# Layer 0's second product in seven block products, with a hand-written order of all engines in that stage

## The chip, the cores and the metric

The kernel runs on one NeuronCore of one Trainium2 chip. The time is the device time of one execution in microseconds (us); a kernel is compared by the median of several executions. The profile records one further execution with the hardware profiler: every instruction of the matrix engine (PE, with its weight loads as PEld), the vector engine (DVE), the scalar engine (ACT), Pool (GpSimd) and the DMA issues of the sync engine's queue (SP). All data are float32.

## The reference, cut to what matters

Four graph layers follow one another over x of shape (128, 64, 256). Only layer 0 is touched:

```python
h = jnp.maximum(_layernorm(x), 0.0)              # 128 * 64 = 8192 rows of 256
agg = jnp.einsum('nm,bmd->bnd', A_hat, h)
x1 = agg.reshape(-1, 256)
h1 = relu(_batchnorm(x1 @ W1.T + b1, g1, be1))   # 512 channels; mean and variance over all rows
out = h1 @ W2.T + b2                             # 256 channels: the second product
out = _batchnorm(out, g2, be2)                   # mean and variance over all rows again
x = x + out.reshape(x.shape)
```

Both batch norms need the statistics of all 8192 rows before any row can go on. Layer 1 (a graph convolution and four LSTMs), layer 2 (attention) and layer 3 (attention with four heads) follow.

## The kernel before, in words

The 8192 rows are cut into 16 chunks of 512 (`CH = 512`, `NCH = 16`). In layer 0 the channels lie on the 128 partitions and the rows of a chunk along the free axis. `KH = 4` blocks of 128 channels make the 512 hidden channels, `KD = 2` make the 256 of the output.

The stage has two passes. In the first, `product1(c)` (line 349) computes z1 of chunk c: its lower two channel blocks go to a tile of the pool `res`, the upper two to a tile of the pool `z1b`; `st1` collects the statistics. Then `bn_params` (line 286) makes scale and shift `sc1`, `sh1`, one channel block after the other.

In the second pass `product2(chunks, by_block)` (line 366) does three things for a chunk: ACT applies scale, shift and relu to the four blocks of z1 into a tile `h1` (line 373; two buffers in the pool `l0b`); PE multiplies by `w2_sb`, two output blocks of four products each (line 377); DVE takes the statistics of each result from PSUM and then writes it to SBUF with the bias added (lines 381 and 382; the result overwrites the lower z1 tile, `z2[c] = lo`). Chunks 0 and 1 are done together, the products ordered by channel block, because their scale and shift come out one block after the other; chunks 2 to 15 one at a time. A float32 matmul of 128x128 weights and 512 columns leaves two records on PE in the trace.

Beside this pass the weights of later layers are prepared. `weight_sums(p, q)` (line 493) loads one of twelve sets of LSTM weights to SBUF (two DMAs on SP, two buffers), lets Pool form four sums or differences of 128x256 (line 502), and stores the set to DRAM (two DMAs, lines 504 and 505); it is called once before each of the chunks 2 to 13. `weight_transposes` (line 463) transposes the weights of layer 2 on PE before chunk 14; `weight_products` follows the last chunk. Then `bn_params` with `st2` makes `sc2`, `sh2`.

What comes next on SP: the weights of layer 1 (`wg0`, `wg1`, `wih1`), then six of the stored sets (`load_sets(6)`, line 549), then the x of chunks 0 and 1 (line 611). The tiles for these lie on the bytes of tiles that the second pass has finished with, `z1b` above all, so each load waits for the last reader of the bytes below it. `first_convolutions` (line 608) starts layer 1: ACT and DVE scale the first chunks with `sc2`, `sh2`, PE transposes them, and DVE adds the x that was loaded (line 622).

The order of the work: inside `tc.manual_schedule(engines=...)` the engines listed issue their instructions in the order of the program text. The other engines' order is made by a planner, which goes by its own estimate of when an instruction can start. Around the second pass only PE is in the list; DVE, ACT, Pool and SP are the planner's. `tc.no_sync_barrier()` is a fence for the planner: no instruction of any engine moves across it, and no engine waits at it. PSUM has eight banks here, one tag `ps`, handed out in turn.

In layer 3 the kernel already computes one product in seven block products (`seven`, line 1308; `sums_h`, line 1298; `ring_places`), with the helper `differences` (line 690): for two-by-two blocks of both factors, four differences on each side replace the eighth product. The LSTMs use the same scheme.

## Time and profile before

| | us |
|---|---|
| median of 5 runs | 1919.75 |
| lowest and highest | 1919.26, 1920.34 |
| the profiled execution's own time | 1919.35 |
| its span, first to last instruction | 1917.5 |

Where the second pass lies in that span, and how busy the engines are in it (us of each window; all at a granted PE clock of 1.00):

| window (us from the span's start) | what | PE | DVE | ACT | Pool |
|---|---|---|---|---|---|
| 157.70 to 171.43 | chunks 2 and 3 | 13.73 | 6.70 | 7.13 | 5.60 |
| 185.17 to 198.90 | chunks 6 and 7 | 13.73 | 5.40 | 5.86 | 6.17 |
| 226.37 to 240.10 | chunks 12 and 13 | 13.73 | 5.39 | 5.86 | 0.00 |
| 240.10 to 253.84 | transposes, chunk 14, most of 15 | 13.73 | 8.01 | 2.93 | 0.08 |

How to read it: the window's length is 13.73 us in each row, so PE has work all the time, and the others wait for it. The sum of an engine's busy time says nothing of the path that sets the end; the chain of waits does. Busy time of PE is modelled from start and size of its matmuls, so rates are better taken from the distance between starts.

### The profile page before, as it was taken

How to read it: one execution, taken by the hardware profiler on the slowest of the kernel's cores; microseconds unless marked ns; L12 is line 12 of the kernel's file. 1: busy time of each engine (PE TensorE's matmuls, PEld its weight loads, DVE VectorE, ACT ScalarE, POOL GpSimd, SP SyncE). 2: the span in 40 equal slices, each digit the busy share in tenths (PEclk: the TensorE clock that was granted, in tenths of full speed). 3: DMA queues.
4: the chain of work that ended last, by engine and by line, in shares of the span. 5: the costliest groups of instructions: out<-in, count | busy, mean ns of one | idle time of the engine just before them, and what ended most of it. 6: DMA issues, size and time to landing. Idle time of an engine off the chain costs nothing.

```text
span 1917.5 us, 38323 instructions
## 1 busy us (share of the span) xinstructions
PE 1898.3 (99%) x14981; PEld 1460.6 (76%) x14981; DVE 1158.2 (60%) x3020; ACT 958.7 (50%) x2132; POOL 414.8 (22%) x615
## 2 busy tenths in 40 slices
PE   9999999999999999999999999999999999999998
PEld 5444465897897889699689789879969967777776
DVE  6644354546557656755755665665555557777776
ACT  5654434445456455455545545545554544444453
POOL 4205210221211121122121121112112213233232
PEclk9999999999999999999999999999999999999999
DMA  4206712224524521532542452253144245444533
GB/s 138 67 32 224 279 49 67 83 83 161 159 83 146 180 99 58 179 105 94 186 144 83 160 182 84 75 197 111 55 160 127 92 131 156 133 142 147 144 111 111
DMA packets 110500, 240.35 MB, mean 125 GB/s; under 512 B 11377, under 2 KB 74353, under 8 KB 110321
## 3 DMA queue, kind: packets, MB, share of 16 engines
q1 hardware_dynamic: 109568, 236.57, 37.1%
q8 instruction: 118, 1.93, 0.4%
q0 software_dynamic: 320, 1.05, 0.2%
q14 instruction: 62, 0.50, 0.1%
q10 hardware_dynamic: 432, 0.30, 0.0%
HBM read 169.98 MB, written 67.90 MB: 124 GB/s over the span
## 4 chain that ended last, share of the span: by engine, by line
PE 94%; DVE 3%; ACT 1%; DMA 1%; issue 0%; POOL 0%; SPq 0%; DVEq 0%; ACTq 0%; POOLq 0%
PE x L848 23%; PE g L812 18%; PE z L848 11%; PE y L848 6%; PE z L377 6%; PE v L1120 6%; PE z L360 5%; PE p_q L1127 3%; PE u L593 3%; PE v L579 3%; PE X L1316 3%; PE Y L1316 1%; PE agg_c L214 1%; PE o L1241 1%; PE agg_b L214 1%; PE o L1443 1%
## 5 line engine op out<-in xcount | busy, mean ns | idle before, releaser
L857 DVE TENSOR_TENSOR gates<-gates,x 128x128 f32<-128x128 f32 (+2 forms) x384 | 119.5, 322 | 335.8 <-PE x L848 333.6
L848 PE MATMUL x<-xd,wset 128*128 128x128 f32 (+2 forms) x1280 | 285.0, 310 | 0.1
L848 PE MATMUL x<-hd,wset 128*128 128x128 f32 (+2 forms) x1152 | 246.7, 303 | 0.0
L906 POOL TENSOR_TENSOR gates<-gates 128x512 f32<-128x512 f32 (+2 forms) x48 | 75.0, 1562 | 647.9 <-ACT gates L740 647.9
L848 PEld LDWEIGHTS x<-xd,wset 128*128 128x128 f32 x1280 | 202.1, 190 | 16.9 <-DVE gates L857 3.0
L740 ACT ACTIVATE gates<-gates,bias 128x256 f32<-128x256 f32 (+4 forms) x384 | 170.4, 490 | 66.4 <-DVE gates L857 63.5
L848 PEld LDWEIGHTS x<-hd,wset 128*128 128x128 f32 x1152 | 185.1, 191 | 5.0
L791 ACT ACTIVATE gates<-g,bias 128x512 f32<-128x512 f32 (+2 forms) x240 | 138.2, 610 | 98.0 <-PE g L812 94.7
L812 PE MATMUL g<-hT,wset 128*128 128x256 f32 (+2 forms) x744 | 184.4, 405 | 1.1 <-DVE hT L751 1.1
L812 PEld LDWEIGHTS g<-hT,wset 128*128 128x128 f32 x744 | 140.5, 190 | 44.1 <-issue 8.8
L812 PE MATMUL g<-hT,wih 128*128 128x512 f32 x384 | 166.4, 592 | 0.0
L854 ACT COPY gates<-y 128x128 f32<-128x128 f32 (+2 forms) x192 | 54.2, 294 | 204.9 <-PE y L848 204.4
L848 PE MATMUL z<-hs,wset 128*128 128x128 f32 (+2 forms) x768 | 154.1, 303 | 0.0
L812 PEld LDWEIGHTS g<-hT,wih 128*128 128x128 f32 x384 | 72.3, 190 | 87.7 <-issue 83.2
L848 PEld LDWEIGHTS z<-hs,wset 128*128 128x128 f32 x768 | 119.8, 191 | 3.3
L360 PE MATMUL z<-agg,w_sb 128*128 128x512 f32 x256 | 114.1, 598 | 0.0
L797 DVE TENSOR_TENSOR cell<-gates 128x512 f32<-128x512 f32 (+2 forms) x80 | 50.6, 650 | 101.2 <-ACT gates L791 101.1
L377 PE MATMUL z<-h,w_sb 128*128 128x512 f32 x256 | 110.2, 592 | 0.0
L857 DVE TENSOR_TENSOR gates<-gates,z 128x128 f32<-128x128 f32 (+2 forms) x384 | 104.6, 316 | 0.1
L854 ACT COPY gates<-x 128x128 f32<-128x128 f32 (+2 forms) x192 | 56.6, 296 | 93.7 <-PE x L848 93.0
L740 ACT ACTIVATE gates<-x,bias 128x128 f32<-128x128 f32 (+2 forms) x192 | 74.8, 390 | 50.9 <-PE x L848 48.0
L848 PE MATMUL z<-hT,wset 128*128 128x128 f32 (+1 forms) x512 | 96.9, 301 | 0.0
(245 smaller groups left out, 3640.5 us busy)
## 6 DMA issues: line engine op xcount, KB each, us to landing
wset<-wfar SPq DMA_DIRECT2D x96, 960.0 KB, 6.4
hT<-far_h SPq DMA_DIRECT2D x124, 128.0 KB, 2.9
far_h<-hm SPq DMA_DIRECT2D x16, 512.0 KB, 4.1
far_n<-xs SPq DMA_DIRECT2D x16, 512.0 KB, 6.4
xs<-far_n SPq DMA_DIRECT2D x64, 128.0 KB, 3.6
far_x<-xs SPq DMA_DIRECT2D x16, 512.0 KB, 3.0
x<-far_x SPq DMA_DIRECT2D x64, 128.0 KB, 3.2
xt<-in_x_dram SPq DMA_DIRECT2D x15, 512.0 KB, 4.0
```

Source lines behind the costliest of these rows:

```text
L360: nc.tensor.matmul(ps, w1_sb[:, k, m * P : (m + 1) * P], agg[:, k, :], start=(k == 0), stop=(k == KD - 1))
L377: nc.tensor.matmul(banks[c, m], w2_sb[:, k, m * P : (m + 1) * P], h1[c][:, k, :], start=(k == 0), stop=(k == KH - 1))
L579: nc.tensor.matmul(banks[m], wg0_sb[:, k, m * P : (m + 1) * P], agg[:, k, :], start=(k == 0), stop=(k == KD - 1))
L740: nc.scalar.activation(gate(q, c, part), src, AF.Tanh if q == 2 else AF.Sigmoid, bias=bs[:, q * KD + c : q * KD + c + 1])
L791: nc.scalar.activation(columns_of(gate(q, c)), natural(banks[q, c][:, :n].rearrange("p (w b) -> p w b", b=nb)), AF.Tanh if q == 2 else AF. ...
L812: nc.tensor.matmul(banks[q, c][:, :n].rearrange("p (w b) -> p w b", b=nb)[:, w, :], block(q, c, k), hv[:, k, w.start * p : (w.stop - 1) * ...
L848: nc.tensor.matmul(folded(self.psum(kind)), wsets[p, self.q][:, BLOCKS[kind][i], :], (ox[self.s] if part == "x" else oh)[kind], start=firs ...
L854: nc.scalar.copy(gate(self.q, kind // 5, halves[kind // 5]), self.psum(kind))
L857: nc.vector.tensor_add(gate(self.q, *dst), gate(self.q, *a), self.psum(kind))
L906: nc.gpsimd.tensor_mul(gates[:, 0, :, :n], gates[:, 0, :, :n], gates[:, 2, :, :n])
L1120: nc.tensor.matmul(ps[:, i, :], hT[:, k, j, :], w[:, k, first : first + D], start=(k == 0), stop=(k == KD - 1))
L1316: nc.tensor.matmul(st[c, tag][:, i * CH // 2 : (i + 1) * CH // 2].rearrange("p (a n) -> p a n", n=P), w, st[c, "o7"][kind], start=first an ...
```

## The change

The second product of chunks 2 to 14 is computed in seven block products instead of eight. The two factors are cut in two by two blocks: the weights into two halves of the 512 hidden channels and two halves of the 256 outputs, the chunk into the two halves of the hidden channels and two halves of 256 rows. A block product has a depth of 256, so two matmuls of 128x128 weights and 256 columns.

- Four combinations of the weight blocks (`w2_sums`) are made once by Pool, in the first pass.
- For each chunk four differences of the blocks of h1, t1 to t4, each 128x512: three on DVE, t3 on Pool (the new argument `third` of `differences`).
- The relu is applied in place, to z1, by ACT (`relu`), no longer into an `h1` tile; the tile of the differences takes the `h1` tag's two buffers.
- The seven products go to three PSUM banks X, Y and Z of a chunk. X is summed on through products 1, 6, 7 and 4 and read after each (`copy` by ACT, `add` by DVE); Y takes products 5 and 3, Z takes 2.
- The statistics are taken from the SBUF result after the bias was added, so `bn_params` runs with `biased` true. Those of chunks 0 and 1 are taken in iterations 3 and 4.
- PE, DVE, ACT and Pool have a hand-written order in this stage, between two fences. Products 7 and 4 of a chunk stand among the first products of the next one. Weight transposes stand around the last two products of chunk 14.
- Chunk 15 keeps the old product, after the second fence; its relus stand on ACT at the end of iteration 14. SP is still the planner's, but its instructions don't cross the fences either.

The core of the diff:

```diff
+    def differences(engine, dst, b11, b12, b21, b22, third=None):
+        t1, t2, t3, t4 = dst
+        return [lambda: engine.tensor_tensor(t1, b12, b11, OP.subtract),
+                lambda: ((third or engine).tensor_tensor(t3, b22, b12, OP.subtract),
+                         engine.tensor_tensor(t2, b22, t1, OP.subtract)),
+                lambda: engine.tensor_tensor(t4, b21, t2, OP.subtract)]
...
-        for c in chunks:
-            for m in range(KD):
-                nc.vector.bn_stats(st2[:, m, c, :], banks[c, m])
-                nc.vector.tensor_scalar(z2[c][:, m, :], banks[c, m], bn2_sb[:, 0, m : m + 1], None,
-                                        op0=OP.add)
+        return banks
+
+    def result2(c, m, ps):
+        nc.vector.tensor_scalar(z2[c][:, m, :], ps, bn2_sb[:, 0, m : m + 1], None, op0=OP.add)
+
+    def stats2(c, m):
+        nc.vector.bn_stats(st2[:, m, c, :], z2[c][:, m, :])
...
+    class Seven2:
+        def __init__(self, c):
+            self.c, self.banks = c, {}
+            self.b = {(k, j): a[:, :, halves2[j]] for k, a in enumerate(z1whole[c]) for j in range(2)}
+
+        def relu(self, *ks):
+            for k in ks:
+                one = slice(k, k + 1)
+                nc.scalar.activation(z1[self.c][k], z1[self.c][k], AF.Relu, bias=sh1[:, one],
+                                     scale=sc1[:, one])
+
+        def begin(self):
+            b = self.b
+            t = l0b.tile([P, 4, KH // 2, CH // 2], F32, tag="h1", name=f"t2_{self.c}")
+            t = [t[:, i] for i in range(4)]
+            self.sums = differences(nc.vector, t, b[0, 0], b[0, 1], b[1, 0], b[1, 1], nc.gpsimd)
+            self.at = {1: b[0, 0], 2: b[1, 0], 3: b[1, 1], 4: t[3], 5: t[0], 6: t[1], 7: t[2]}
+
+        def product(self, kind, tag):
+            first = tag not in self.banks
+            if first:
+                self.banks[tag] = bank(f"{tag}2_{self.c}")[:, : CH // 2]
+            for k in range(KH // 2):
...
+                nc.tensor.matmul(self.banks[tag], w, right[:, k, :], start=first and not k, stop=True,
+                                 skip_group_check=True)
+
+        def copy(self, m, j, tag):
+            nc.scalar.activation(self.part(m, j), self.banks[tag], AF.Identity,
+                                 bias=bn2_sb[:, 0, m : m + 1])
+
+        def add(self, m, j, tag):
+            nc.vector.tensor_add(self.part(m, j), self.part(m, j), self.banks[tag])
+
+        def stats(self, m):
+            nc.vector.bn_stats(st2[:, m, self.c, :], z2[self.c][:, m, :])
...
+        w2_sums = l0b.tile([P, 4, KH // 2, P], F32, name="w2_sums", bufs=1)
...
+            nc.gpsimd.tensor_tensor(w2_sums[:, dst], u, v, op)
...
-        for c in range(2, NCH):
-            if c == NCH - 2:
-                weight_transposes()
+    tc.no_sync_barrier()
+    with tc.manual_schedule(engines={mybir.EngineType.PE, mybir.EngineType.DVE,
+                                     mybir.EngineType.Activation, mybir.EngineType.Pool}):
+        sevens = {c: Seven2(c) for c in range(2, NCH - 1)}
+        sevens[2].relu(2, 3, 0, 1)
+        for c in range(2, NCH - 1):
+            a, b, z = sevens[c], sevens.get(c + 1), sevens.get(c - 1)
             if wanted:
                 weight_sums(*wanted.pop(0))
-            product2([c], False)
-        sc2, sh2 = bn_params(st2, bn2_sb, const, "bn2", False)
+            a.product(2, "Z")
+            if c == 2:
+                a.begin()
+                for f in a.sums:
+                    f()
+                for m in range(KD):
+                    result2(0, m, banks[0, m])
+            if b:
+                b.relu(0)
+            if z:
+                z.product(7, "X")
+                z.add(1, 1, "X")
+            if b:
+                b.relu(1)
+            a.product(1, "X")
+            a.copy(0, 0, "X")
+            if z:
+                z.stats(0)
+            a.product(5, "Y")
+            a.copy(1, 1, "Y")
+            if b:
+                b.relu(2)
+            a.add(0, 0, "Z")
+            if c == 2:
+                for m in range(KD):
+                    result2(1, m, banks[1, m])
+            if z:
+                z.product(4, "X")
+                z.copy(1, 0, "X")
+            if b:
+                b.relu(3)
+                b.begin()
+                b.sums[0]()
+            if z:
+                z.stats(1)
+            a.product(6, "X")
+            a.copy(0, 1, "X")
+            if b:
+                b.sums[1]()
+            else:
+                new_h1(c + 1)
+                for k in range(KH):
+                    relu2(c + 1, k)
+            a.product(3, "Y")
+            a.add(0, 1, "Y")
+            if b:
+                b.sums[2]()
+            if c in (3, 4):
+                for m in range(KD):
+                    stats2(c - 3, m)
+        weight_transposes(range(2))
+        a.product(7, "X")
+        a.add(1, 1, "X")
+        a.stats(0)
+        weight_transposes(range(2, 3 * KD))
+        a.product(4, "X")
+        a.copy(1, 0, "X")
+        a.stats(1)
+    tc.no_sync_barrier()
+    with tc.manual_schedule(engines={mybir.EngineType.PE}):
+        c = NCH - 1
+        banks = product2([c], False)
+        for m in range(KD):
+            result2(c, m, banks[c, m])
+            stats2(c, m)
+        sc2, sh2 = bn_params(st2, bn2_sb, const, "bn2", True)
         c2_ps = weight_products()
```

`relu2` is the old relu into an `h1` tile, now a function of its own; `part(m, j)` is the block of the result with output block m and row half j.

## The prediction

> **What bounds the kernel now.** First I read the page's busy line and the chain of waits from the end of layer 0's first product to the first convolutions; then the timeline of that stretch, for the period of a chunk and for what the other engines have to spare; last the groups by shape, for prices. (Timeline rows: start, length, engine, operation, and in brackets how long the engine was idle before and what ended that.)

> ```profile
> PE 1898.3 (99%) x14981; PEld 1460.6 (76%) x14981; DVE 1158.2 (60%) x3020; ACT 958.7 (50%) x2132; POOL 414.8 (22%) x615
> ```
> ```profile
> 144.04 96.13 PE z L377 x224
> 240.18 1.31 PE wt L467 x12
> 241.49 13.74 PE z L377 x32
> ```

> The chain is TensorE alone: 256 records of line 377 in 109.87 us, 0.429 each. A float32 matmul leaves two records, so a chunk is 16 records, 6.867 us; the DVE rows below, two chunks apart, say the same (226.48, 240.21: 13.73). In this stretch ACT and DVE are busy some 3 us of every 6.87, and wait for TensorE.

> ```profile
> 226.48 0.70 DVE L381 BATCH_NORM_STATS2 st<-z 128x6 f32<-128x512 f32 x1 [2.08 <-PE z L377]
> 226.54 1.52 ACT L373 ACTIVATE h<-z1a,sh_bn,sc_bn 128x512 f32<-128x512 f32 x2 [3.94 <-PE z L377]
> ...
> 240.21 0.70 DVE L381 BATCH_NORM_STATS2 st<-z 128x6 f32<-128x512 f32 x1 [2.08 <-PE z L377]
> ```

> **The products.** Thirteen chunks (2 to 14) give up 16 records of 512 columns for 7 x 4 records of 256. What four of those cost back to back, layer 3's block products show:

> ```profile
> 1594.13 1.03 PE L1316 MATMUL Z<-hT,w_sb 128*128 128x256 f32 x4
> 1594.99 1.03 PE L1316 MATMUL X<-hT,w_sb 128*128 128x256 f32 x4
> 1595.86 1.89 PE L1120 MATMUL v<-w_sb,hT 128*128 128x256 f32 x8
> ```

> Start to start it is 0.863 us (1595.86 - 1594.13, halved); the weight loads (0.19 a record by their row) fit under the 0.216 of a record. Where a product really waited, its first record took 0.08 to 0.10 more. A chunk is 7 x 0.863 = 6.04 us, so 0.826 is saved, and **13 x 0.826 = 10.7 us**, if nothing else sets the pace.

> **ACT in the new period.** Four in-place relus at 0.72 start to start (1.52 for two, one alone 0.80), and four copies of 128x256 with a bias at 0.47: 4.8 of 6.04. The tight path: product 5 ends at 3.45 of the period, its result is readable 0.20 later (modelled end plus 0.04, as line 381 follows line 377), then copy(1,1), relu 2, copy(1,0) and relu 3 stand in ACT's queue: 0.37 + 0.72 + 0.37 + 0.80 start to start, plus 0.05 to TensorE, ends at 5.96. The next chunk's product 2 needs relu 3 at 6.04. It fits by 0.08, so I charge nothing for it; without it each chunk stalls by what is missing.

> **DVE, and the port it shares with Pool.** Three differences of 128x512 (0.69, as cell<-gates), three adds of 128x256 from PSUM (0.42), two statistics (0.69): 4.7 of 6.04. Pool gets t3 (128x512, 1.27 by the gates row) beside the four weight sums at 0.73: 4.2. But two inputs from SBUF on both engines at once cost:

> ```profile
> L502 POOL TENSOR_TENSOR ws<-ws 128x256 f32<-128x256 f32 x48 | 33.6, 728 | 33.2 <-DMA ws<-in_whh_t_dram 32.3
> L906 POOL TENSOR_TENSOR gates<-gates 128x512 f32<-128x512 f32 x24 | 30.4, 1268 | 255.7 <-ACT gates L740 255.7
> L797 DVE TENSOR_TENSOR cell<-gates 128x512 f32<-128x512 f32 x48 | 32.4, 691 | 55.6 <-ACT gates L791 55.6
> ```
> ```profile
> 1416.59 0.73 POOL L693 TENSOR_TENSOR xd<-hT 128x256 f32<-128x256 f32 x1 [14.36 <-DVE hT L751]
> 1416.81 1.05 DVE L751 TENSOR_TENSOR hT<-gates 128x512 f32<-128x512 f32 x1 [0.30 <-ACT gates L791]
> 1417.94 1.11 POOL L694 TENSOR_TENSOR xd<-hT 128x256 f32<-128x256 f32 x1 [0.62 <-DVE hT L751]
> 1419.01 1.18 POOL L695 TENSOR_TENSOR xd<-hT,xd 128x256 f32<-128x256 f32 x1
> ```

> A DVE operation of 0.69 takes 1.05 and Pool's of 0.73 takes 1.18: one waits for the other. Here t3 and the second difference are both released by relu 3, so they meet each time. Walked through one period: relu 3 at 5.96; second difference, behind t3, until 7.8; add(0,1) 8.2; third difference behind a weight sum 9.0; add(1,1) 9.4; and product 4 of the older chunk wants that bank at 3.45 + 6.04 = 9.49. It just fits; if DVE goes first, it fits by 0.6. With nothing in the way it costs 0; if every difference waits out 0.55, DVE needs 4.7 + 3 x 0.55 = 6.35, plus its own waits, say 6.45, or 5.3 us over thirteen chunks. The walk is nearer the first end: **1.0 us**.

> [...]

> **The edges.**
> - Chunk 2 has no older chunk between its products: ACT's copies and relus of chunk 3 come late, relu 3 about 0.5 after product 3 ends. **0.5** (0 to 1).
> - Chunks 0 and 1 get their statistics in iterations 3 and 4, 1.38 more on a full DVE each; add(1,1) is late, and product 4 behind it, with all of TensorE. **1.5** (0 to 2.8).
> - Bank order: with eight in a ring, chunk 15's first bank is chunk 14's X, which copy(1,0) has only just read: 0.16 + 0.04 + 0.47 + 0.05. **0.7** (0 to 0.75).
> - The last chunk adds the bias before its statistics. Before, DVE ran statistics, bias add, aggregate; now the first two swap, and one small add of 0.16 goes: **-0.2**.
> - Pool's four sums of w2 (2.9) lie in the first product's stage, where Pool sits idle 6.64 before its rstd of 27.65. 0; without that cover up to 2.9.
> - Transposes, relus of chunks 0, 1 and 15 and the bias adds are the same number of instructions, elsewhere in order: 0.

> **SP's queue and the DMAs.** The twelve weight sets keep their loads and stores, but Pool now does one set a chunk, each behind a t3. Before, the last set's store went out at 217.13, and everything queued on SP behind it followed:

> ```profile
> 217.13 0.32 SPq L504 DMA_DIRECT2D wfar<-ws  x1
> ...
> 221.66 10.33 SPq L549 DMA_DIRECT2D wset<-wfar  x6
> 243.23 0.93 SPq L611 DMA_DIRECT2D early<-in_x_dram  x2
> ...
> 261.05 0.69 DVE L622 TENSOR_TENSOR xs<-early,at_b 128x512 f32<-128x512 f32 x1 [1.81 <-PE at_b L239]
> ```

> The two-microsecond windows have the DMA engines full from 217 to 227 (that store, the small weights, the first set: 3.3 MB) and from 231 to 242 (the five other sets). Now the last set belongs to iteration 13, which begins at about 157.8 + 0.5 + 11 x 6.04 = 224.7; t3 and four sums with some waits end near 230. Then 10.1 and 11.5 us of transfers, and 1.7 for x: x lands near 253.3. DVE wants it at 261.05 less the gain, 253.8 for 7.2. The old slack of 13 us is gone. **0.5** (0 if sets come early, 5 if each is late).

> **Sum:** -10.7 + 1.0 + 0.5 + 1.5 + 0.7 - 0.2 + 0.5 = -6.7. The profiled execution took 1919.35 (span 1917.5 and 1.85 around it), so 1912.65; the median of the runs, 1919.75, lies 0.4 higher: **1913.0 us**.

> **The rivals.**
> - *DVE and Pool set the pace.* For: the rows above, and both engines some 70% full. Against: only three of eight DVE operations take two inputs from SBUF. Period 6.45: 13 x 0.42 = 5.4, less 2.5 for the edges: 1916.9.
> - *The x load ends last.* A set's buffer went round in 11.8 to 13.0 us before (Pool's starts at 162.49, 174.37, 186.53, 198.33, 211.33), two sets a round; two new periods are 12.1. At 12.8 the sets are 4 us late at the end, x lands at 257, and only 4 us of gain remain: 1915.7. Against: each store and load now has the queue more to itself.
> - *Slower: the loads fall behind the stores.* SP's order is the planner's. If it keeps two stores and then two loads (as at 165.41 to 173.31), the load of a set stands behind the next set's store, and that behind a t3. Two sets then cost 4.8 (load) + 2.9 + 1.3 + 2.9 + 0.8 (store) + 3.3 (six waits for the port) = 16, or 8.0 a chunk; t3 comes late, product 7 waits, and TensorE behind it. Six pairs are 96 against 82.4 before; less 5.5 of slack that t3 has, plus edges, some 9.5 us slower: 1929. It decides once a set takes over 6.87. Against: a store becomes ready six microseconds after the last one, and the next load before that.

> **How the numbers follow.** Forecast 0.62, DVE and Pool 0.17, x late 0.11, slower 0.10. 0.2% (3.84 us) is about what a measurement of this kernel can tell from no change. Faster by more: 0.60 of the first, 0.06 and 0.08 of the next two, 0.74; within it 0.02 + 0.09 + 0.03 = 0.14; slower 0.12. The range: all of 10.7 gives 1909.0, rival one with edges on the dear side 1918.5; what it leaves out is mostly the slower case.

> **What would show it.** Right: 28 records a chunk at 0.216 and product 2 starting every 6.0 to 6.2 us from chunk 4; waits at product 4 in iterations 3 and 4 alone; DVE differences of 0.7 to 1.8 and Pool's t3 beside them; the last wfar store near 230; TensorE waiting once for ACT before chunk 15. Wrong: product 7 waiting for Pool (the slower case), product 2 for ACT in each iteration (its path is longer than 2.5), product 4 for DVE in each (the port), or the first xs add waiting for a DMA.

## The result, and the profile after

The changed kernel takes 1923.86 us (median of 25 runs, 1922.71 to 1926.22) against 1919.72 us for the kernel before (43 runs, 1918.94 to 1921.51). The ratio is 1.0022, with a 95% interval of 1.0016 to 1.0027: **slower by some 4 us**, where 1913.0 was forecast. The profiled execution took 1924.06 us.

The page's busy line of the changed kernel (busy us, share of the span, instructions):

```profile
PE 1890.8 (98%) x15137; PEld 1489.7 (77%) x15137; DVE 1188.0 (62%) x3070; ACT 979.4 (51%) x2184; POOL 445.0 (23%) x632
```

TensorE has 7.5 us less to do than before (1898.3) and yet the span is 4.8 longer. So the products were saved; TensorE now stands still. Where, is read from three points that both traces have: the first record of the second product, the first record of `weight_products` (right behind the last chunk) and the first product of layer 1's LSTM (`g<-hT`).

| | before | after | difference |
|---|---|---|---|
| second product begins | 143.88 | 144.95 | +1.07 |
| `weight_products` begins | 255.06 | 252.02 | -3.04 |
| first LSTM product | 286.92 | 291.28 | +4.36 |
| end of the span | 1917.5 | 1922.3 | +4.8 |

The stage itself gained 4.11 us (111.18 to 107.07). The piece behind it, between the second and third point, lost 7.40 (31.86 to 39.26), and that piece wasn't changed at all. After it another 0.44 is lost, in small pieces.

**The stage.** From one chunk's product 2 to the next one's it is 6.04 us in the undisturbed iterations, as forecast. In two iterations it is 7.86 and 7.92. The timeline of the changed kernel around the second of these (start, length, engine, line; in brackets how long the engine was idle before and what ended that):

```profile
216.22 0.38 SPq L573 DMA_DIRECT2D ws<-in_wih_t_dram  x1
...
218.32 0.32 SPq L581 DMA_DIRECT2D wfar<-ws  x1
...
219.17 0.90 SPq L573 DMA_DIRECT2D ws<-in_whh_t_dram  x1
...
223.24 2.99 POOL L579 TENSOR_TENSOR ws<-ws 128x256 f32<-128x256 f32 x4 [3.71 <-DMA ws<-in_whh_t_dram]
...
226.18 1.72 POOL L309 TENSOR_TENSOR t<-z1b,z1a 128x512 f32<-128x512 f32 x1
...
227.93 0.47 ACT L439 ACTIVATE z1a<-Y,bn_sb 128x256 f32<-128x256 f32 x1 [3.09 <-POOL t L309]
...
228.46 1.13 PE L432 MATMUL Y<-z1b,w_sums 128*128 128x256 f32 x4 [1.58 <-ACT z1a L439]
```

Read it from the top. The first half of a weight set was issued at 216.22. The second half (219.17) comes 2.95 us later, because SP's order has the store of another set between the two halves, and that store waits for Pool. So Pool gets the set at 223.24 only, after 3.71 us of waiting, and t3 stands behind the four sums in Pool's hand-written order: it runs from 226.18 to 227.90. ACT's copy(1,1) then waits for t3: it writes over the block of z1 that t3 still reads. Product 3 goes on in the bank that copy(1,1) reads, so TensorE stops.

**Behind the stage.** The same kernel, SP's queue after the last weight set and what waits for it:

```profile
238.65 0.32 SPq L581 DMA_DIRECT2D wfar<-ws  x1
...
264.52 0.69 DVE L769 TENSOR_TENSOR xs<-early,at_b 128x512 f32<-128x512 f32 x1 [7.96 <-DMA early<-in_x_dram]
...
269.00 2.39 PE L214 MATMUL agg_b<-adjt_bd,cv 64*64 64x64 f32 x64 [7.61 <-ACT cv L187]
```

and the longest piece of its chain of waits there (start, length, what):

```profile
248.80 15.60 DMA early<-in_x_dram
```

Before, the last store of a set went out at 217.13; now at 238.65. The sets follow from 244.29 on, and the x of the first chunks, issued behind them at 248.80, lands 15.60 us later. DVE's first xs add waits 7.96 us for it, and TensorE is idle for 7.61 us. Before, the longest of the two waits at the same place was 1.1 (us in total, times, longest):

```profile
PE agg_b L214 <- ACT cv L187: 1.3, 2, 1.1
```

### The profile page after: what moved, and what is told of

It is laid out like the page before. It is cut to its first block, busy times and chain, and to the rows that moved or that the text cites. A ratio compares the mean times of both kernels' runs of the same rounds, so it can differ in the third digit from the quotient of the medians.

```text
span 1922.3 us, 38825 instructions
## 1 busy us (share of the span) xinstructions
PE 1890.8 (98%) x15137; PEld 1489.7 (77%) x15137; DVE 1188.0 (62%) x3070; ACT 979.4 (51%) x2184; POOL 445.0 (23%) x632
## 3 DMA queue, kind: packets, MB, share of 16 engines
q0 software_dynamic: 320, 1.05, 0.2%
## 4 chain that ended last, share of the span: by engine, by line
PE 83%; DVE 2%; DMA 1%; ACT 1%; issue 0%; SPq 0%; POOL 0%; DVEq 0%; ACTq 0%; POOLq 0%
PE x L987 23%; PE g L951 18%; PE z L987 11%; PE y L987 6%; PE v L1259 5%; PE p_q L1266 3%; PE u L740 3%; PE v L726 3%; PE X L1455 3%; PE Y L1455 1%; PE agg_b L214 1%; PE agg_c L214 1%; PE o L1380 1%; PE o L1582 1%; PE s L1349 1%; DMA early<-in_x_dram 1%
## 5 line engine op out<-in xcount | busy, mean ns | idle before, releaser
L369 PEld LDWEIGHTS z<-agg,w_sb 128*128 128x128 f32 x256 | 47.3, 190 | 54.6 <-issue 51.2
```

The costliest lines, as they stand in the source:

```text
L369: nc.tensor.matmul(ps, w1_sb[:, k, m * P : (m + 1) * P], agg[:, k, :], start=(k == 0), stop=(k == KD - 1))
```

## The experiments

All are compared with the kernel before on the same chip. Beside each time stand the two distances that the table above is made of: to the start of `weight_products`, and from there to the first LSTM product (in the profiled execution); "rest" is from there to the end of the span. The median is of all executions, the distances are of one, which in e1 and e4 took 2.1 above and 1.9 below the median and in e10 1.6 below it.

| kernel | median us | ratio to before (95%) | to `weight_products` | to LSTM | rest |
|---|---|---|---|---|---|
| before | 1919.7 to 1920.0 | | 255.06 | 31.86 | 1630.6 |
| after | 1923.86 | 1.0022 (1.0016 to 1.0027) | 252.02 | 39.26 | 1631.0 |
| e1_x_first | 1916.45 | 0.9981 (0.9973 to 0.9990) | 252.73 | 33.03 | 1631.0 |
| e3_t3_on_dve | 1916.77 | 0.9982 (0.9973 to 0.9991) | 247.67 | 35.07 | 1633.1 |
| e4_busy_fill | 1922.78 | 1.0015 (1.0006 to 1.0024) | 250.57 | 38.32 | 1630.2 |
| e5_sums_alone | 1920.53 | 1.0005 (0.9995 to 1.0014) | 255.71 | 32.94 | 1630.9 |
| e6_t3_x | 1916.20 | 0.9980 (0.9970 to 0.9990) | 247.83 | 31.87 | 1633.6 |
| e7_sp_by_hand | 1912.07 | 0.9959 (0.9947 to 0.9972) | 246.88 | 33.05 | 1630.4 |
| e8_all | 1914.99 | 0.9975 (0.9965 to 0.9985) | 247.86 | 31.87 | 1634.2 |
| e9_before_x | 1920.47 | 1.0003 (0.9994 to 1.0012) | 255.31 | 31.87 | 1631.4 |
| e10_sp_alone | 1916.04 | 0.9981 (0.9972 to 0.9990) | 246.46 | 35.68 | 1630.5 |
| e11_sp_edges | 1911.08 | 0.9952 (0.9939 to 0.9964) | 246.57 | 31.88 | 1631.1 |
| e12_sp_t3_dve | 1914.79 | 0.9973 (0.9963 to 0.9983) | 248.15 | 31.87 | 1633.1 |

**e1_x_first: the x ahead of the sets.** The changed kernel, with the six sets loaded after the x:

```diff
-    load_sets(6)
 ...
+            if n == 2:
+                load_sets(6)
```

> The changed kernel with one thing moved: the two loads of x stand on SP ahead of the six weight sets (load_sets(6) is emitted two steps into the next stage). Theory A (x is late because it stands behind six sets of 0.98 MB in SP's queue and in the DMA engines): the loads go out when the last z1b tile is free, near 245, land near 249, the first xs add comes at its transposes, near 258 instead of 264.5, TensorE's idle 7.6 us goes and with it the fall of its clock: about 8 us off the changed kernel's 1923.9, so 1916, 4 below the kernel before. Rival (x waits for its bytes or for the store of the last set, not for the sets): it lands near 262 as before and the time stays 1923 to 1924. Rival (the sets, now later, are missed at line 951 near 305): the gain is given back there.

1916.45 us: 7.4 less than the changed kernel. The distance to the LSTM falls from 39.26 to 33.03, and the stops in the stage stay (2.91 and 0.81 us, both before product 3). The late x is a cost of its own. **e9_before_x**, the same edit on the kernel before, is the control:

> The kernel before with the x loads ahead of the six sets. There the x landed and DVE's first xs add waited for TensorE, not for a DMA. If the x load is a cost of the changed kernel alone: the same time as before, 1919.3 to 1920.1. If x ahead of the sets also shortens something later (the six sets are not needed soon, but other loads are): faster by 1 or more, and the gain of the x edit in the changed kernel, 7.4 us, isn't all the late x.

It changes nothing that can be told (1920.47, the interval holds 1). The order of x and sets cost nothing before; the change made it dear.

**e3_t3_on_dve: the t3 of the changed kernel on DVE.**

```diff
-            self.sums = differences(nc.vector, t, b[0, 0], b[0, 1], b[1, 0], b[1, 1], nc.gpsimd)
+            self.sums = differences(nc.vector, t, b[0, 0], b[0, 1], b[1, 0], b[1, 1])
```

> The changed kernel with t3 on DVE instead of Pool. Theory B (Pool's queue couples TensorE to the weight loads: t3 stands behind four weight sums that wait for a DMA, copy(1,1) may not write over what t3 reads, and product 3 waits for copy(1,1)): the two stops of 1.7 us before product 3 and the two of 0.37 behind them vanish, Pool's sets run ahead by themselves, the last store goes out near 220 and x is there in time; 4 us off the stage and 6 to 8 off its end, so 1913 to 1916. Rival (the port and DVE set the pace): DVE has four differences of 0.69 a chunk, 5.4 us and waits for the port in 6.04, product 4 waits for DVE in most chunks, 0.3 to 0.5 each, and what the sets give is spent: 1918 to 1921.

1916.77: between the 1913 to 1916 that was expected and the rival's 1918 to 1921. The stops before product 3 are gone, the last store goes out at 228.11, and the stage ends 4.35 us earlier (247.67). The x is still late, by 2.98 us by its wait. DVE, with one difference more, doesn't set the pace.

**e4_busy_fill: TensorE kept busy.** While it waits for the x, TensorE has 84 transposes of nothing instead of 16. This asks what the half clock behind the wait costs.

```diff
-            for at, fill, name in ((6, 16, "d"), (9, 6, "e"), (10, 6, "f")):
+            for at, fill, name in ((6, 84, "d"), (9, 6, "e"), (10, 6, "f")):
```

> The changed kernel with 84 instead of 16 idle transposes (0.109 us each) between the first transposes of layer 1 and its first aggregation, so that TensorE works through the 7.6 us in which it waits for x; nothing else. Theory C (the pause also halves the granted clock until 274, which costs what the same 64 + 6 + 8 records take longer, 0.4 + 0.6 + 0.35 us): 1.3 us off, so 1922.6, with the clock at 1.0 throughout. Rival (the slow records only fill time in which TensorE waits for DVE and ACT anyway): 1923.5 to 1924.

1922.78. The clock stays at 1.00, and the distance to the LSTM is 0.94 shorter: about 1 us of the loss was clock, the rest the wait. In the time alone that can't be told, for the intervals of this kernel and the changed one overlap.

**e5_sums_alone: the kernel before, with the four sums of w2 on Pool added** (lines 503 to 508 of the changed kernel; nothing reads them).

> The kernel before with one part of the change alone: Pool forms the four sums of w2 in the first product's stage, and nobody reads them. Theory (Pool's first sum holds the port at 24.8 to 25.5, DVE's two masks beside it take 0.82 instead of 0.29, and DVE's statistics, Pool's rstd and the third aggregation follow 0.53 later): 0.5 us slower than before, 1920.2. Rival (Pool's idle time hides them, and the 0.53 in the profile comes of the late first x like the 0.54 before it): 1919.7.

The time, 1920.53, can't be told from before: its interval holds 1. The trace shows the cost nevertheless. In the timeline of this kernel:

```profile
24.35 0.83 DVE L144 TENSOR_SCALAR mask<-adj_bd 64x64 f32<-64x64 f32 x2
24.36 1.45 POOL L443 TENSOR_TENSOR w_sums<-w_sb 128x256 f32<-128x256 f32 x2 [3.22 <-DMA w_sb<-in_w2t_dram]
```

and in that of the kernel before:

```profile
24.23 0.29 DVE L144 TENSOR_SCALAR mask<-adj_bd 64x64 f32<-64x64 f32 x2
```

Two small masks take 0.83 instead of 0.29 beside Pool's first sum. In the changed kernel, where the same two take 0.82, the first of them takes 0.19 and the second ends at 25.59, with that sum (25.55). DVE is late by 0.54, and all of the first product behind it. Pool's idle time did hide Pool's work, but not what that work did to DVE.

**e6_t3_x: both edits**, t3 on DVE and x first.

> The changed kernel with both edits: t3 on DVE, and both x loads issued ahead of the six sets. If the two losses are separate causes: the t3 edit alone left 2.6 us of TensorE idle before agg_b and two steps of half clock (6.83 us of records, so about 3.4 us lost); the x edit removes the first (the xs add no longer waits for a DMA) and part of the second. 1916.8 - 2.6 - 1 to 3 = 1911 to 1913. If instead the x load only takes over a wait that something else sets at the same place (at_b transposes, ACT's scaling), it stays at 1915 to 1917. Stage period 6.04 in most chunks, no stop before product 3.

1916.20: a miss. Up to the LSTM the expectation holds (247.83 and 31.87, the first LSTM product 11.6 us earlier than in the changed kernel), so each edit takes away a loss that the other leaves. They overlap (e1 was 5.5 earlier there, e3 8.5), for t3 on DVE also brings the x earlier. But 2.6 us are lost in the rest, 1633.6 against 1631.0. Where, shows in layer 3, in stops of TensorE that nothing ends ("issue"). The last section comes back to them.

**e7_sp_by_hand: SP's order.** x first as in e1, t3 left on Pool. SP joins the engines whose order is written out; the load of a set is split off and goes out two iterations ahead, both halves together, behind the store that frees its buffer.

```diff
-        def weight_sums(p, q):
-            w = stage.tile([P, 16, P], F32, tag="ws", name=f"ws_{p}_{q}", bufs=2)
+        held = {}
+        def weight_load(p, q):
+            w = held[p, q] = stage.tile([P, 16, P], F32, tag="ws", name=f"ws_{p}_{q}", bufs=2)
...
+        def weight_sums(p, q):
+            w = held.pop((p, q))
...
-                                     mybir.EngineType.Activation, mybir.EngineType.Pool}):
+                                     mybir.EngineType.Activation, mybir.EngineType.Pool,
+                                     mybir.EngineType.SP}):
+        for o in wanted[:2]:
+            weight_load(*o)
...
             if wanted:
                 weight_sums(*wanted.pop(0))
+                if len(wanted) > 1:
+                    weight_load(*wanted[1])
```

> The changed kernel with x ahead of the sets, t3 left on Pool, and SP's order by hand: the load of a weight set goes out two iterations ahead, after the store of the set before the last, so no load stands behind the next set's store. Theory 'late loads' (Pool's t3 is late because four sums ahead of it wait for a set that SP issued behind a store): the stops before product 3 go, the last wfar store comes before 232, and the time is 1912 to 1914, as with t3 on DVE and x first. Rival 'Pool itself' (t3 stands behind four sums of 3.7 to 4.2 us that the port stretches; the loads only add to it): the stops of 0.4 to 1.7 us stay at some chunk, time 1915 to 1917, as with x first alone (1916.45).

1912.07, 7.8 us faster than before and 11.8 than the changed kernel. From iteration 6 on every chunk takes 6.04, with t3 on Pool. Its timeline, for the same steps as above:

```profile
206.75 1.28 POOL L309 TENSOR_TENSOR t<-z1b,z1a 128x512 f32<-128x512 f32 x1 [0.94 <-ACT z1b L411]
...
207.98 3.70 POOL L584 TENSOR_TENSOR ws<-ws 128x256 f32<-128x256 f32 x4
...
210.47 0.47 ACT L439 ACTIVATE z1a<-Y,bn_sb 128x256 f32<-128x256 f32 x1 [0.40 <-PE Y L432]
```

Pool's sums wait for no DMA, though four of them take 3.70 beside DVE's differences (in the kernel before one took 0.728 on average, so four 2.91): both halves of their set are in SBUF by then, and those of a later one go out side by side at 210.04 and 210.47. t3 ends at 208.03, 2.44 us before copy(1,1), which now waits for TensorE alone. So Pool wasn't too slow; it was fed too late.

**e10_sp_alone: e7 with the x left behind the sets.**

> SP's order by hand as in e7_sp_by_hand, t3 on Pool, but the x loads left behind the six sets. If the loads behind the stores are the one root, and the late x only follows from the late last store: the last wfar store comes near 230 as in e7, x is in time, and the time is e7's, 1912 to 1913. If x behind the sets is a cause of its own in a shorter stage: as with t3 on DVE alone (last store 228.5, x landed at 255.2, TensorE idle 2.6 us, two steps of half clock), 3 to 5 us above e7: 1915 to 1917.

1916.04. SP's order alone brings the stage to 246.46, and the last store to 229.59. The x, issued at 239.25, comes late all the same, as its timeline shows:

```profile
229.59 0.32 SPq L586 DMA_DIRECT2D wfar<-ws  x1
...
255.99 0.69 DVE L779 TENSOR_TENSOR xs<-early,at_b 128x512 f32<-128x512 f32 x1 [4.97 <-DMA early<-in_x_dram]
```

So there are two causes, and each edit alone brings 7 to 8 us: SP's order removes both stops (4.6 us of the stage) and lets DVE begin on the x 8.5 earlier; x first removes the wait for it whatever the stage does. Together, in e7, they bring 11.8, as part of the wait is taken away by either.

**e12_sp_t3_dve: e7 with t3 on DVE**, for the miss of e6.

> e7_sp_by_hand with t3 on DVE. e6_t3_x reached layer 1 0.3 us before e7, and then lost 3.2 us in layer 3, in two stops of TensorE that nothing in the profile ends. If these belong to the program with t3 on DVE (its instructions stand elsewhere): 1914 to 1916, with such stops in layer 3 again. If they belong to e6's order on SP or to chance: within 1 us of e7, 1911 to 1913.

1914.79. At the LSTM it stands where e7 does (280.02 against 279.93); the rest is 2.7 us longer, with a stop of 1.45 us in layer 3. The loss goes with t3 on DVE, not with SP's order.

**e8_all and e11_sp_edges: the edges.** To e6 and to e7 two edits are added: the statistics of chunks 0 and 1 are spread over iterations 6 to 9, and the four sums of w2 are formed after chunk 3 of the first product, behind a fence.

```diff
-            if c in (3, 4):
-                for m in range(KD):
-                    stats2(c - 3, m)
+            if 6 <= c < 10:
+                stats2((c - 6) // 2, c % 2)
```

> The t3 and x edits, and two smaller ones: the statistics of chunks 0 and 1 are taken one per iteration in iterations 6 to 9 instead of four in iterations 3 and 4, and Pool's four sums of w2 come later in the first product's stage, away from the mask on DVE. If the edges cost what the trace shows (0.2 and 1.0 us before product 4 in iterations 3 and 4 with t3 on DVE, and 0.5 at the mask): 1.2 to 1.7 us faster than the kernel with the two edits alone, so 1910 to 1911.5. If the stops at the edges only move to the spread statistics: the same as that kernel.

> e7_sp_by_hand with the statistics of chunks 0 and 1 one per iteration in iterations 6 to 9 and Pool's four sums of w2 later in the first product's stage. In e7 the stops before product 4 in iterations 3 to 5 are 0.65, 0.90 and 0.28; the second and third go with the statistics (1.2), and the mask gives 0.5: 1910 to 1911. In e8_all, where t3 was on DVE, the second and third stop went too, but two new ones of 0.83 and 0.63 came, when Pool's sums met DVE; if that happens here also, 1911.5 to 1912.5.

e8 (1914.99) missed its 1910 to 1911.5. It is 1.2 faster than e6, the near end of the gain expected, but the intervals overlap: the stop of 1.04 in iteration 4 went, and two of 0.83 and 0.63 came before product 4 in later iterations; its stage ends where e6's does (247.86), though the masks gave their 0.5 here too: its first product had begun 0.69 later than e6's. In e11, with t3 on Pool, the stops of 0.90 and 0.28 went and only one of 0.58 came in iteration 8. The masks take 0.29 again. It takes **1911.08 us**, 0.9952 of the time before (0.9939 to 0.9964): faster than both kernels, and the lowest median of the study. Against e7 it can't be told by the intervals; and of the 1.5 us by which it reaches the LSTM earlier than e7, 1.2 are a step of half clock that e7 had there and e11 hadn't (last section). Of its waits of TensorE between the second product and the LSTM one is left that the kernel before hadn't (us in total, times, longest):

```profile
PE X L432 <- DVE z1a L443: 0.7, 2, 0.4
```

It is that for DVE's add, ahead of product 4.

## Why the prediction was wrong

Its sum was -6.7, against +4.7 in the profiled executions. By its own steps:

- **The products** (-10.7): right. 6.04 us a chunk in undisturbed iterations, in e7 and e11 almost throughout. (The two starts that the prediction halves give 0.865, not 0.863, and so 10.5; the chunks themselves show 0.863.)
- **ACT's path** (0, "it fits by 0.08"): right. In e7 product 2 waits for no relu after chunk 3.
- **The port** (1.0): mis-sized, nothing. The port is the prediction's name, and the expectations', for what makes DVE and Pool slow each other down; no run shows what they share. What the runs show is longer operations, as expected (in the changed kernel's stage t3 took 1.54 on average and 1.27 at the least, a weight sum 0.89 and 0.72, the differences on DVE 0.67 to 1.65; DVE's adds, 0.40 to 0.42, and its statistics, 0.68 to 0.70, didn't grow). But e7 shows a steady 6.04 with all that, and not the 6.45 of the rival. The rival in which DVE and Pool set the pace is refuted, by e3 too.
- **The edges:** chunk 2, 0.5 forecast, 0.13 measured. Statistics of chunks 0 and 1, 1.5 forecast, 1.35 measured (stops of 0.65 and 0.70 before product 4 in iterations 3 and 4), and e11 shows that they caused only the second: with the statistics moved away, the first stays at 0.65. Bank order, 0.7 forecast, nothing measured: chunk 15's sixteen records stand 0.43 apart and begin 0.87 after product 4. The tail's -0.2 isn't seen either: from `weight_products` to the first at_b transpose it is 5.23, before 5.24.
- **The sums of w2** (0, "up to 2.9" without cover): the cover named was the wrong one. Pool had the time; the price, 0.53 in the changed kernel, is paid by DVE, whose two masks take 0.82 there beside Pool's first sum and 0.29 before.
- **SP's queue and the DMAs** (0.5, "5 if each is late"): **the step that failed.** It took 7.40, and in three ways. The last store was put "near 230" and came at 238.65, because t3 and the weight sets held each other up; with SP's order by hand alone it is 229.59. The transfers from there to the landing of x were put at 10.1 + 11.5 + 1.7 = 23.3; they took 25.8 in the changed kernel and 26.3 in e10. So even with the store on time e10's x let DVE begin at 255.99, not 253.3, when DVE wanted it near 252.5. About 1 us of the 7.40 was half clock, which no step had.
- **The two stops in the stage**: 4.60 us (1.81 at product 3 and 0.47 at the next product 2 in one, 1.85 and 0.47 in the other), in no step. They come from the rival's "5.5 of slack that t3 has". That was counted to product 7, which *reads* t3. But t3 reads a block that copy(1,1) overwrites half an iteration earlier (in e7 at 210.47, product 7 at 213.67); the slack in e7 is 2.44 us.

Of what is left, 0.54 at the very start is a first x that landed later; over the runs here the first product of the first pass begins anywhere from 13.47 to 14.65. Some 0.5 in the stage, most of it first records that took 0.10 longer, and 0.44 behind the first LSTM product stand in no step.

**The rivals.** "The x load ends last" assumed sets 4 us late and x at 257; it was 8.7 late against the same 230, and x came at 264.4. "The loads fall behind the stores" named the mechanism, a load behind the next set's store, but held for half a load, and cost two stops instead of 8.0 us a chunk; the argument against it, that "the next load before that" is ready, overlooked that an order once written is kept, ready or not. The two were weighed as separate cases of 0.11 and 0.10, each with the other one's harm left out. They came together: a store ahead of half a load makes the load late, the load the sums and t3 behind them, the sums the next store, and the last store the x. And the x is late even without that, as e10 shows. With SP's order and the x mended, e7 and e11 land at 1912.07 and 1911.08, within 2 us of the forecast: the gain was there, and the queue gave it back. That they land so near is in part luck: e7's stage is 8.7 us shorter than before, where the sum without SP's queue and the tail had 7.0, and 1.2 of that 1.7 was lost again to a step of half clock, which the sum hadn't.

## What to carry to other kernels

When an operation joins an engine's hand-written order, list everything that stands ahead of it there and what that waits for, down to the DMA queue: an operation of 1.3 us behind four sums is only as punctual as the load that feeds them. Take its slack to the first instruction that *overwrites* one of its inputs, not only to the first that reads its result. And when a stage gets shorter, the transfers that lay hidden behind it must be timed anew, with the stage's new end as the date and the last transfer queued ahead as the start: the x had 13 us to spare, and an order that cost nothing then cost 7 us.

## What the runs showed of the hardware that wasn't expected

**A half clock in steps.** Windows of the changed kernel behind the wait for x (busy us of each engine with instructions in parentheses; then granted clock, DMA share, GB/s):

```profile
262.00:264.00 2.00, 0.00 (x0) 0.00 (x0) 0.00 (x0) 0.00 (x0) 0.00 (x0) 0.92 1.02 324
...
272.00:274.00 2.00, 2.00 (x7) 1.33 (x6) 1.90 (x7) 0.13 (x1) 0.71 (x1) 0.52 0.00 0
```

0.92 in a window of 2 us is 0.32 us at half clock, 0.52 is 1.92; with the four windows between, all at 0.50, that makes 10.24 us. In e3 it is 6.83 us, and in e7, at the same place but after an idle time of only 1.09 us, 3.4 (0.97 and 0.75 in two windows of 6 us): near to three, two and one of the same length. The table shows what one such step costs there: the distance to the LSTM is 31.86 to 31.88 in six kernels (in the kernel before, e11 and e12 the clock is 1.00 all the way), and 33.03, 32.94 and 33.05 in e1, e5 and e7, with a step of 3.4 each: 1.1 to 1.2 us more. An idle time of 1.1 us at this place was followed by a step in e1, e5 and e7 and by none in the kernel before, e11 and e12. What brings a step on, and why they have this length, no run here shows.

**Stops in layer 3.** In all four kernels with t3 on DVE (e3, e6, e8, e12) TensorE stops for 1.0 to 1.5 us between 1601 and 1605, within a row of 64 like products, 60 or 61 of them done, and waits for nothing that the profile shows. The timeline of e12:

```profile
1599.78 1.10 PE L1545 MATMUL s<-qk 64*64 64x64 f32 x60
...
1602.33 0.33 PE L1545 MATMUL s<-qk 64*64 64x64 f32 x4 [1.45 <-issue]
```
